# Moving the layer norm's factor from the output onto the queries, in a four-layer kernel on one core

## The chip, the core and the metric

The kernel runs on one core of a Trainium2 chip. The core has five engines with queues of their own: TensorE (PE in the profile, with its weight loads as PEld), VectorE (DVE), ScalarE (ACT), GpSimd (POOL) and SyncE (SP), which here only issues DMAs. The metric is the time on the device in microseconds, as the median of several runs.

## The reference

The input is a batch of 16 images of 4096 tokens (64 x 64) with 256 channels. Four layers follow each other, each as `x = x + layer(group_norm(x))`: a search in a codebook of 1024 entries, an attention along image rows with a sigmoid, a gate from a softmax over all tokens of an image, and a linear attention with a layer norm. The change concerns the last one:

```python
qkv = einsum('bxyc,cf->bxyf', x, w_qkv); q, k, v = split(qkv, 3)      # 4 heads of 32
q = softmax(q, over the 32) * 32 ** -0.5
k = softmax(k, over the 4096 tokens)
context = einsum('bhdn,bhen->bhde', k, v)
out = einsum('bhde,bhdn->bhen', context, q)
out = einsum('bxyh,hc->bxyc', out, w_out) + b_out
mu, var = mean and variance of out over the 256 channels
out = (out - mu) * rsqrt(var + 1e-3) * gamma + beta
```

The layer's result is added to its input, and the sum is the kernel's output.

## The kernel before

All work is cut into chunks of 512 tokens (`NCHUNK` = 8 chunks per image, `CH` = 4 tiles of 128 tokens per chunk). Each image goes through generators: `stats0` and `stage1` (the search), `layer1`, `rows2`, `stage2` and `gate2` (the gate), and `stage3` (the last layer). The generators of up to five images run interleaved. At the end of `tile_net_kernel` a heap of tasks decides the interleaving (L890 to L920): a task has a start, a length and a total, and each `yield n` of its generator moves it on by `length * n / total`. So an image's `stage3` is issued in pieces between the pieces of other stages of later images. Each engine works through its own queue in order, and one engine's wait holds all that is queued behind it, of whatever stage. SP issues most of the loads and stores, and its queue is in order too.

`stage3` has two loops over the chunks. The first (L740 to L801) makes the softmax of the keys, the context, and the queries. `queries` (L722) transposes the normalized queries of a chunk to 128 rows (4 heads x 32) by 512 tokens and stores them to DRAM. Between the loops (L803 to L827) the context is folded with `w_out` into one matrix of 128 x 256, `wctx`, whose second half carries gamma. Since `w_out` and the bias are centred over the channels in advance, the mean of the layer norm is zero. The variance of a token is then a quadratic form in its query, with the matrix `gram`.

The second loop (L854 to L882) is the output loop. Its parts are:

- `form(ch)` (L832) loads the transposed queries of a chunk again (L834, SP), multiplies them with `gram` (L836, PE) and multiplies the result by the queries (L838, DVE).
- `variance(ch)` (L840) sums over the 128 rows with four one-column matmuls (L844, PE), adds the epsilon (L846, ACT) and raises to the power -0.5 on POOL (L847). This gives the layer norm's factor, one number for each token, in `rss[ch]`, with the tokens along the partitions.
- For each pair of token tiles (`pr`), two products of queries and `wctx` go into one PSUM bank, `po` (L864). Each of the two is copied to the output tile `y` by ACT, which multiplies by the factor as a scale for each partition (L867).
- The residual input, stored with channels along the partitions, is transposed by PE into a second bank, `px` (L869), and a matmul of one row (L873) adds beta and what the group norm takes off.
- One pair later, DVE adds `px` to `y` (L875; the last one in L883), and SP stores a finished `y` (L878, L884).

Within the output loop a pair's step also carries the `form` (first pair) or the `variance` (second pair) of the next chunk.

PSUM is allocated from two pools: `ps_m` with four buffers of one bank each, which nearly all of the above draws from in turn (`bank`), and `ps_w` with two buffers of two banks. The queries' tile `qo` has three buffers, and `y` (tag `u4`) two.

Of the kernel before, what the change touches and what calls it, by code (L numbers as in the profile page):

```python
# [12 lines left out]
AF = mybir.ActivationFunctionType  # L13
ALU = mybir.AluOpType
AX = mybir.AxisListType

P = 128
C = 256
# [3 lines left out]
CH = 4  # L22
NCHUNK = NT // CH
# [18 lines left out]
def kernel(  # L42
# [7 lines left out]
    nc = tc.nc  # L50
# [17 lines left out]
    def bank(name):  # L68
        return ps_m.tile([P, 512], F32, tag="pm", name=name)
# [5 lines left out]
    ident = const.tile([P, P], F32, name="ident")  # L75
# [64 lines left out]
    def twice(row):  # L140
        return row.unsqueeze(1).to_broadcast([P, 2, C])
# [45 lines left out]
    for hf in range(2):  # L187
        pe = bank(f"pe_{hf}")
        for k in range(NK):
            nc.tensor.matmul(  # L190
                pe, lhsT=neg_mat, rhs=e_sq[:, k, hf * 512 : (hf + 1) * 512],
                start=(k == 0), stop=(k == NK - 1),
# [54 lines left out]
    for n in range(4):  # L247
        t = const.tile([P, 8], F32, name=f"m8_{n}")
# [450 lines left out]
    def stage3(b):  # L699
        tag = f"s3_{b}"  # L700
        dst = out[b].rearrange("(t p) c -> p t c", p=P)
        x3 = x3_d.pop(b)
        scale, nmean, xm_ = norm3.pop(b)
# [36 lines left out]
        for ch in range(NCHUNK):  # L740
# [23 lines left out]
            for pr in range(CH // 2):  # L764
                pqv = bank(f"pqv_{tag}_{ch}_{pr}").rearrange("p (j n) -> p j n", j=2)
                for j in range(2):
                    t = 2 * pr + j
                    for k in range(NK):
                        nc.tensor.matmul(  # L769
                            pqv[:, j, :], lhsT=xt[:, k, t * P : (t + 1) * P], rhs=wqv_n[:, k, :],  # L770
                            start=(j == 0 and k == 0), stop=False, skip_group_check=True,
# [33 lines left out]
        with tc.high_priority(offset=URGENT):  # L805
# [8 lines left out]
            wctx = wts.tile([P, 2, C], F32, tag="wctx", name=f"wctx_{tag}")  # L814
# [14 lines left out]
        queries(NCHUNK - 1)  # L829
        qs, prods, rss = {}, {}, {}  # L830

        def form(ch):  # L832
            qs[ch] = s3p.tile([P, CW], F32, tag="qo", name=f"qo_{tag}_{ch}", bufs=3)
            nc.sync.dma_start(out=qs[ch], in_=qTs[ch])  # L834
            pz = bank(f"pz_{tag}_{ch}")
            nc.tensor.matmul(pz, lhsT=gram, rhs=qs[ch], start=True, stop=True)  # L836
            prods[ch] = s3p.tile([P, CW], F32, tag="v2", name=f"qz_{tag}_{ch}", bufs=4)
            nc.vector.tensor_tensor(prods[ch], pz, qs[ch], ALU.mult)  # L838

        def variance(ch):  # L840
            prod = prods.pop(ch)
            pv = bank(f"pvr_{tag}_{ch}")
            for t in range(CH):
                nc.tensor.matmul(pv[:, t : t + 1], lhsT=prod[:, t * P : (t + 1) * P], rhs=one, start=True, stop=True)  # L844
            rss[ch] = small.tile([P, CH], F32, tag="ln_rs", name=f"lrs_{tag}_{ch}")
            nc.scalar.activation(rss[ch], pv[:, 0:CH], AF.Identity, bias=eps3)  # L846
            nc.gpsimd.tensor_tensor(rss[ch], rss[ch], mhalf, ALU.pow)  # L847

        form(0)
        yield 3  # L850
        variance(0)
        yield 3
        before = late = None
        for ch in range(NCHUNK):  # L854
            xt = xb.tile([P, NK, CW], F32, tag="xb", name=f"xo_{tag}_{ch}")
            nc.sync.dma_start(out=xt, in_=x3[ch])
            qT, rs = qs.pop(ch), rss.pop(ch)
            y = s3p.tile([P, CH, C], F32, tag="u4", name=f"y_{tag}_{ch}")
            for pr in range(2):
                po = bank(f"po_{tag}_{ch}_{pr}").rearrange("p (j c) -> p j c", c=C)  # L860
                px = bank(f"pxo_{tag}_{ch}_{pr}").rearrange("p (j c) -> p j c", c=C)
                for j in range(2):
                    t = 2 * pr + j
                    nc.tensor.matmul(  # L864
                        po[:, j, :], lhsT=qT[:, t * P : (t + 1) * P], rhs=wctx[:, 1, :], start=True, stop=True
                    )
                    nc.scalar.activation(y[:, t, :], po[:, j, :], AF.Copy, scale=rs[:, t : t + 1])  # L867
                    for k in range(NK):
                        nc.tensor.matmul(  # L869
                            px[:, j, k * P : (k + 1) * P], lhsT=xt[:, k, t * P : (t + 1) * P], rhs=ident,  # L870
                            is_transpose=True, start=(j == 0 and k == 0), stop=False, skip_group_check=True,
                        )
                nc.tensor.matmul(px, lhsT=ones3, rhs=twice(x_row), start=False, stop=True, skip_group_check=True)  # L873
                if late is not None:
                    nc.vector.tensor_tensor(late[1], late[0], late[1], ALU.add)  # L875
                late = px, y[:, 2 * pr : 2 * pr + 2, :]
                if pr == 1 and before is not None:
                    nc.sync.dma_start(out=dst[:, (ch - 1) * CH : ch * CH, :], in_=before)  # L878
                if ch + 1 < NCHUNK:
                    (form, variance)[pr](ch + 1)  # L880
                yield 3
            before = y  # L882
        nc.vector.tensor_tensor(late[1], late[0], late[1], ALU.add)  # L883
        nc.sync.dma_start(out=dst[:, TOK // P - CH :, :], in_=before)  # L884


# [28 lines left out]
    while queue:  # L915
        now, n = heapq.heappop(queue)
        _, length, gen, total = tasks[n]
# [39 lines left out]
```

## Time and profile before

| | |
|---|---|
| median of 3 runs | 5826.19 us (5826.03 to 5828.86) |
| profiled execution, its own time | 5832.41 us |
| span of the profiled execution | 5830.7 us |
| mean granted TensorE clock | 0.951 |
| DMA moved | 1059.49 MB, 182 GB/s over the span |
| `stage3` of the first image: first and last output addition | 1015.9 and 1114.0 us |
| output loop of the last image | 5784.3 us to the end |

The profiled execution is one run under the hardware profiler, and the times of single instructions come from it. A line of the groups reads: line of the kernel, engine, operation, output tile and input tiles, their shapes, how often; then busy us and mean ns of one; then the idle time of the engine just before these instructions, with what ended most of it. A line of the chain of work names the engine and the work that the end of the kernel was waiting for at that time. A line of the timeline has start, duration, engine, line, operation and tiles. A line of the waits names who waited for what: us in total, times, longest.

### The profile page before, as it was taken

The numbers are of one execution on the slowest core, as the hardware profiler recorded it, in microseconds if no ns is written. First come the engines' busy times: TensorE is split into PE (matmuls) and PEld (weight loads), VectorE is DVE, ScalarE is ACT, GpSimd is POOL, SyncE is SP. The second block draws the span as 40 slices with busy tenths as digits, with TensorE's granted clock in tenths as the row PEclk, the third lists the DMA queues.
The fourth block names the chain that finished last, engine by engine and source line by source line (L and its number), as shares of the span: only waits on it lengthen the run. The fifth ranks groups of instructions, "written<-read, shape, count | busy, mean of one in ns | idle before, by whom it ended". The sixth has DMA issues, their size and how long they took to land.

```text
span 5830.7 us, 79945 instructions
## 1 busy us (share of the span) xinstructions
PE 5289.1 (91%) x28463; PEld 3208.3 (55%) x28463; DVE 5145.4 (88%) x7282; ACT 4565.2 (78%) x6754; POOL 1956.8 (34%) x1314
## 2 busy tenths in 40 slices
PE   8978899889999999999999999999999999987778
PEld 3534455545656556565655656565565655564555
DVE  6489798899999999999999989999998999998883
ACT  4477597878878787887878788787888878888873
POOL 3123234223343333433333343332424334331332
PEclk9988999989999999999999999999999999998889
DMA  6443746555665656566565656657565664644543
GB/s 186 140 150 107 254 112 192 188 166 173 199 195 179 224 155 210 180 199 202 175 221 166 205 188 199 204 161 231 160 206 178 197 215 137 217 163 173 189 145 127
DMA packets 521381, 1059.49 MB, mean 182 GB/s; under 512 B 52504, under 2 KB 266392, under 8 KB 512792
## 3 DMA queue, kind: packets, MB, share of 16 engines
q1 hardware_dynamic: 406288, 885.11, 44.8%
q0 software_dynamic: 73728, 67.14, 8.0%
q10 hardware_dynamic: 40968, 102.13, 4.7%
q8 instruction: 226, 3.70, 0.3%
q14 instruction: 171, 1.40, 0.1%
HBM read 751.18 MB, written 303.04 MB: 181 GB/s over the span
## 4 chain that ended last, share of the span: by engine, by line
PE 36%; DVE 18%; ACT 12%; issue 5%; DMA 4%; POOL 3%; ACTq 0%; SPq 0%; POOLq 0%; DVEq 0%
PE pd_s L387 11%; DVE ex_s L630 8%; ACT ex_s L627 5%; PE po_s L864 3%; PE ph_l L477 3%; PE po_l L515 2%; PE pqv_s L769 2%; PE pk_s L747 2%; DVE i_s L398 2%; POOL qv_s L789 2%; PE pz_s L836 2%; PE pvr_s L844 1%; DVE nn_s L393 1%; PE pxo_s L869 1%; ACT nn_s L382 1%
## 5 line engine op out<-in xcount | busy, mean ns | idle before, releaser
L630 DVE CUSTOM_DVE_ANT_0 ex_s<-ex_s,x2b 128x2048 f32<-128x2048 f32 x1024 | 2392.9, 2343 | 73.4 <-ACT ex_s L627 72.8
L627 ACT ACTIVATE ex_s<-x0b,nmax_s,x_r 128x2048 f32<-128x2048 f32 x1024 | 2138.4, 2089 | 49.1 <-DVE num_s L630 40.0
L387 PE MATMUL pd_s<-e,xn_s 128*128 128x512 f32 x4096 | 2007.4, 622 | 64.5 <-DVE m L393 53.2
L399 POOL DMA_INDIRECT xc_s<-in_emb_rows,i_s x512 | 1121.4, 2190 | 1785.4 <-DVE i_s L398 1188.4
L387 PEld LDWEIGHTS pd_s<-e,xn_s 128*128 128x128 f32 x4096 | 760.2, 198 | 822.3 <-issue 681.3
L393 DVE CUSTOM_DVE_ANT_0 nn_s<-pd_s,nn_s 128x1024 f32<-128x1024 f32 x512 | 619.9, 1212 | 190.2 <-PE pd_s L387 91.7
L398 DVE FIND_INDEX8 i_s<-m,nn_s 128x8 uint32<-128x1024 f32 x512 | 623.0, 1217 | 0.1
L382 ACT ACTIVATE nn_s<-ne,nx_s 128x1024 f32<-128x1024 f32 x512 | 581.8, 1143 | 43.6 <-DVE nx_s L353 20.6
L477 PE MATMUL ph_l<-wh_l,xt_l 128*128 128x256 f32 x2048 | 533.4, 395 | 17.9 <-DVE m L393 12.5
L769 PE MATMUL pqv_s<-wqv_s,xk_s 128*128 128x256 f32 x2048 | 490.2, 381 | 0.0
L477 PEld LDWEIGHTS ph_l<-wh_l,xt_l 128*128 128x128 f32 x2048 | 382.0, 194 | 137.8 <-issue 64.4
L769 PEld LDWEIGHTS pqv_s<-wqv_s,xk_s 128*128 128x128 f32 x2048 | 389.3, 191 | 120.1 <-issue 58.0
L847 POOL TENSOR_TENSOR lrs_s<-lrs_s,mhalf 128x4 f32<-128x4 f32 x128 | 165.5, 1293 | 746.2 <-ACT lrs_s L846 720.1
L867 ACT ACTIVATE y_s<-po_s,lrs_s 128x256 f32<-128x256 f32 x512 | 239.1, 472 | 186.7 <-PE po_s L864 128.2
L864 PE MATMUL po_s<-wctx_s,qo_s 128*128 128x256 f32 x1024 | 335.1, 417 | 32.0 <-ACT y_s L867 30.5
L789 POOL TENSOR_TENSOR qv_s<-qv_s,qm_s 128x512 f32<-128x512 f32 x128 | 202.4, 1581 | 353.7 <-DVE qm_s L788 185.0
L515 PE MATMUL po_l<-at_l,h_l 64*128 64x64 f32 x4096 | 308.8, 286 | 7.5 <-DVE m L393 4.9
L515 PEld LDWEIGHTS po_l<-at_l,h_l 64*128 64x128 f32 x4096 | 272.1, 194 | 75.4 <-issue 37.1
L738 POOL TENSOR_TENSOR qv_s<-qv_s,qd_s 128x512 f32<-128x512 f32 x128 | 210.6, 1645 | 281.8 <-DVE qd_s L737 151.5
L864 PEld LDWEIGHTS po_s<-wctx_s,qo_s 128*128 128x128 f32 x1024 | 177.0, 198 | 175.6 <-ACT y_s L867 85.4
L332 ACT ACTIVATE xn_s<-xt_s,nb_n,s_n 128x512 f32<-128x512 f32 x256 | 200.7, 808 | 73.5 <-PE pd_s L387 48.5
L747 PE MATMUL pk_s<-xk_s,wk_s 128*128 128x512 f32 x512 | 253.3, 618 | 1.5 <-DMA xk_s<-x_g 1.2
(200 smaller groups left out, 7451.9 us busy)
## 6 DMA issues: line engine op xcount, KB each, us to landing
xs_s<-in_xT SPq DMA_DIRECT2D x128, 512.0 KB
xt_s<-in_xT SPq DMA_DIRECT2D x128, 512.0 KB
xc_s<-in_x SPq DMA_DIRECT2D x128, 512.0 KB
x_s<-xt_s ACTq DMA_DIRECT2D x128, 512.0 KB
xt_l<-x_s SPq DMA_DIRECT2D x128, 512.0 KB
x_l<-xt_l SPq DMA_DIRECT2D x128, 512.0 KB
xr_r<-x_l SPq DMA_DIRECT2D x128, 512.0 KB
xg_g<-x_l SPq DMA_DIRECT2D x128, 512.0 KB
```

The source lines that it names most:

```text
L382: nc.scalar.activation(nn, ne2, AF.Identity, bias=nx2[ch][:, t : t + 1])
L387: nc.tensor.matmul(pd[:, cols], lhsT=xn[ch][:, k, t * P : (t + 1) * P], rhs=e2[:, k, cols], start=(k == 0), stop=(k == NK - 1),)
L393: nc.vector.tensor_tensor_reduce(out=nn, in0=pd, in1=nn, scale=1.0, scalar=-3.0e38, op0=ALU.add, op1=ALU.max, accum_out=m8[:, 0:1],)
L398: nc.vector.max_index(i8, m8, nn)
L399: nc.gpsimd.indirect_dma_start(out=xc[ch][:, t, :], out_offset=None, in_=emb_rows, in_offset=bass.IndirectOffsetOnAxis(ap=i8[:, 0:1], axis=0),
L477: nc.tensor.matmul(ph[:, t, :], lhsT=X[:, k, t * P : (t + 1) * P], rhs=wh_n[:, k, :], start=(t % 2 == 0 and k == 0), stop=False, skip_grou ...
L515: nc.tensor.matmul(po[:, r, k * CH + t, :], lhsT=h[rows, t, k * P : (k + 1) * P], rhs=at[rows, t, :], start=True, stop=True,)
L627: nc.scalar.activation(ex, x0b, AF.Exp, bias=nmax[:, T : T + 1], scale=x01[:, T, 1:2], accum_out=den[:, h, T : T + 1])
L630: nc.vector.tensor_tensor_reduce(out=ex, in0=ex, in1=x2b, scale=1.0, scalar=0.0, op0=ALU.mult, op1=ALU.add, accum_out=num[:, h, T : T + 1],)
L747: nc.tensor.matmul(pk, lhsT=wk_n[:, k, :], rhs=xt[:, k, :], start=(k == 0), stop=(k == NK - 1))
L769: nc.tensor.matmul(pqv[:, j, :], lhsT=xt[:, k, t * P : (t + 1) * P], rhs=wqv_n[:, k, :], start=(j == 0 and k == 0), stop=False, skip_group ...
L864: nc.tensor.matmul(po[:, j, :], lhsT=qT[:, t * P : (t + 1) * P], rhs=wctx[:, 1, :], start=True, stop=True)
```

## The change

The factor is no longer a scale in the eviction of the products. A new function, `deviate`, spreads it: four PE transposes of a column broadcast over 128 columns give a bank in which each token's factor stands in all 128 rows, and DVE multiplies the queries by that bank. The products, the transposes of the residual and the row then go into one bank, as one accumulation, and ACT copies it to `y` in one instruction per pair. The additions on DVE are gone.

The loading of the queries becomes a function of its own, `fetch`, which runs three chunks ahead of the outputs; `form` and `variance` run two chunks ahead, and `deviate` one. Ahead of the loop stand three loads, two forms, two variances and one `deviate`, with steps between them. `qs` keeps its three buffers.

```diff
-        def form(ch):
+        def fetch(ch):
             qs[ch] = s3p.tile([P, CW], F32, tag="qo", name=f"qo_{tag}_{ch}", bufs=3)
             nc.sync.dma_start(out=qs[ch], in_=qTs[ch])
+
+        def form(ch):
             pz = bank(f"pz_{tag}_{ch}")
...
+        def deviate(ch):
+
+            rs = rss.pop(ch)
+            pd = bank(f"pdv_{tag}_{ch}")
+            for t in range(CH):
+                nc.tensor.transpose(pd[:, t * P : (t + 1) * P], rs[:, t : t + 1].to_broadcast([P, P]), ident)
+            nc.vector.tensor_tensor(qs[ch], pd, qs[ch], ALU.mult)
+
+        fetch(0)
+        fetch(1)
         form(0)
         yield 3
         variance(0)
-        yield 3
-        before = late = None
+        fetch(2)
+        yield 2
+        form(1)
+        yield 2
+        deviate(0)
+        variance(1)
+        yield 2
+        before = None
         for ch in range(NCHUNK):
             xt = xb.tile([P, NK, CW], F32, tag="xb", name=f"xo_{tag}_{ch}")
             nc.sync.dma_start(out=xt, in_=x3[ch])
-            qT, rs = qs.pop(ch), rss.pop(ch)
+            qT = qs[ch]
             y = s3p.tile([P, CH, C], F32, tag="u4", name=f"y_{tag}_{ch}")
             for pr in range(2):
-                po = bank(f"po_{tag}_{ch}_{pr}").rearrange("p (j c) -> p j c", c=C)
+                if pr == 1 and ch + 1 < NCHUNK:
+                    deviate(ch + 1)
                 px = bank(f"pxo_{tag}_{ch}_{pr}").rearrange("p (j c) -> p j c", c=C)
                 for j in range(2):
                     t = 2 * pr + j
-                    nc.tensor.matmul(
-                        po[:, j, :], lhsT=qT[:, t * P : (t + 1) * P], rhs=wctx[:, 1, :], start=True, stop=True
-                    )
-                    nc.scalar.activation(y[:, t, :], po[:, j, :], AF.Copy, scale=rs[:, t : t + 1])
                     for k in range(NK):
                         nc.tensor.matmul(
                             px[:, j, k * P : (k + 1) * P], lhsT=xt[:, k, t * P : (t + 1) * P], rhs=ident,
                             is_transpose=True, start=(j == 0 and k == 0), stop=False, skip_group_check=True,
                         )
+                for j in range(2):
+                    t = 2 * pr + j
+                    nc.tensor.matmul(
+                        px[:, j, :], lhsT=qT[:, t * P : (t + 1) * P], rhs=wctx[:, 1, :], start=False, stop=False,
+                        skip_group_check=True,
+                    )
                 nc.tensor.matmul(px, lhsT=ones3, rhs=twice(x_row), start=False, stop=True, skip_group_check=True)
-                if late is not None:
-                    nc.vector.tensor_tensor(late[1], late[0], late[1], ALU.add)
-                late = px, y[:, 2 * pr : 2 * pr + 2, :]
-                if pr == 1 and before is not None:
-                    nc.sync.dma_start(out=dst[:, (ch - 1) * CH : ch * CH, :], in_=before)
-                if ch + 1 < NCHUNK:
-                    (form, variance)[pr](ch + 1)
+                nc.scalar.copy(y[:, 2 * pr : 2 * pr + 2, :], px)
+                if pr == 0:
+                    if ch + 2 < NCHUNK:
+                        form(ch + 2)
+                else:
+                    if ch + 2 < NCHUNK:
+                        variance(ch + 2)
+                    if ch + 3 < NCHUNK:
+                        fetch(ch + 3)
+                    if before is not None:
+                        nc.sync.dma_start(out=dst[:, (ch - 1) * CH : ch * CH, :], in_=before)
                 yield 3
             before = y
-        nc.vector.tensor_tensor(late[1], late[0], late[1], ALU.add)
         nc.sync.dma_start(out=dst[:, TOK // P - CH :, :], in_=before)
```

## The prediction

> **What bounds the kernel now.** I read the busy shares first, then one stretch in the middle, then the chain of work that ended last, then the groups of the output loop, then that loop instruction by instruction.
>
> ```profile
> PE 5289.1 (91%) x28463; PEld 3208.3 (55%) x28463; DVE 5145.4 (88%) x7282; ACT 4565.2 (78%) x6754; POOL 1956.8 (34%) x1314
> ...
> 2700.00:3000.00 300.00, 283.48 (x1622) 178.36 (x1621) 280.83 (x401) 251.40 (x377) 109.46 (x72) 0.98 0.60 187
> ```
>
> The second line is one 300 us stretch: busy us of PE, weight loads, DVE, ACT, POOL, then granted clock, DMA share, GB/s. PE and DVE both look 94% busy, ACT 84%. For PE that overstates the load. The Trainium skill ("Perfetto Trace Analysis", section Identifying the Most-Contended Engine) says that matmul busy time is a poor measure because matmuls overlap in the pipeline, and that the occupancy of VectorE is a fair one. The trace agrees: a 512-column fp32 pass of L387 is listed with 622 ns, but eight in a row take 3.43 us in the chain, 0.43 us each. At such paces PE's work is 4864 passes of 512 columns x 0.43 = 2092 us, 5120 of 256 columns x 0.216 (eight of L477 in 1.73 us) = 1106 us, and about 1300 us of small ones (5376 of up to 128 columns at 0.11 = 590, the rest the narrow products of attention and the rows): 4500 us, 77% of the span. By the busy row PE binds and every added matmul lengthens the kernel; by the pace DVE is the fullest queue, and PE has room that is lost in waits. I take the pace.
>
> ```profile
> PE 36%; DVE 18%; ACT 12%; issue 5%; DMA 4%; POOL 3%; ACTq 0%; SPq 0%; POOLq 0%; DVEq 0%
> ```
>
> The chain changes engines all the time; no engine alone sets the end. These shares name 78% of the span, so I weigh time saved on PE by 36/78 = 0.46, on DVE by 0.23, on ACT by 0.15. That is my choice of a rule for a kernel of coupled queues.
>
> ```profile
> L864 PE MATMUL po_s<-wctx_s,qo_s 128*128 128x256 f32 x1024 | 335.1, 417 | 32.0 <-ACT y_s L867 30.5
> L867 ACT ACTIVATE y_s<-po_s,lrs_s 128x256 f32<-128x256 f32 x512 | 239.1, 472 | 186.7 <-PE po_s L864 128.2
> L875 DVE TENSOR_TENSOR y_s<-pxo_s,y_s 128x512 f32<-128x512 f32 x240 | 163.0, 680 | 34.1 <-ACT y_s L867 33.6 <-PE pxo_s L873 0.3
> L838 DVE TENSOR_TENSOR qz_s<-pz_s,qo_s 128x512 f32<-128x512 f32 x128 | 87.6, 685 | 75.0 <-PE pz_s L836 73.2 <-DMA qo_s<-qd_s 1.6
> L774 ACT COPY qv_s<-pqv_s 128x512 f32<-128x512 f32 x256 | 142.9, 576 | 39.5 <-PE pqv_s L773 39.3
> ```
>
> The last two figures of a line are the idle time before the group and its main cause. The output loop is a ping-pong: product (PE), scaled eviction (ACT), the next product into the other half of the same bank, eviction again. Both sides wait for each other. In the chain it looks like this:
>
> ```profile
> 2584.84 0.45 PE po_s L864 x2
> 2585.29 0.02 issue
> 2585.31 0.48 ACT y_s L867
> 2585.80 0.04 issue
> 2585.84 0.71 PE po_s L864 x2
> ```
>
> Two passes of a product at full pace take 0.43 us; after such a wait they take 0.6 to 0.7.
>
> **The change part by part.** There are 16 batches x 8 chunks = 128 chunks.
>
> *DVE.* The 256 residual additions go (L875 163.0 + L883 10.8 = 173.8 us). In come 128 products of spread factor and queries, 512 columns with one operand in PSUM, which is L838's shape: 128 x 685 ns = 87.7 us. Work: -86 us. The wait of 33.6 us for ACT goes. The new product waits for its transposes: nothing at best, 75 us at worst (L838's own wait on PE). The transposes stand well before their use, so I take the middle, 37. DVE: -86 - 34 + 37 = -83 us.
>
> *ACT.* The 512 scaled evictions go (239.1 us work, 186.7 us idle before them). In come 256 plain copies of 512 columns out of PSUM, L774's shape: 256 x 576 ns = 147.5 us, with L774's wait of 39.5. ACT: -92 work, -147 waiting, -239 us. Its wait for the POOL power (32.5 us in 25 cases) goes to PE.
>
> *PE.* The products, residual transposes and row are the same instructions, into one bank. Added are four transposes a chunk, 512 in all. The residual transposes give the pace:
>
> ```profile
> 5641.46 0.60 PE L869 MATMUL pxo_s<-ident,xo_s 128*128 128x128 f32 x4
> 5641.90 0.38 PE L873 MATMUL pxo_s<-x_row,ones 128*128 128x512 bf16 x1
> ```
>
> Four start 0.44 us before the next instruction, so 0.11 us each and 512 x 0.11 = +56 us. A broadcast column as weights is not in the trace; if nothing overlapped it would be 512 x 0.288 (mean of the transposes L362) = 147 us. I take 56, the same instruction but for the operand's step. Removed are PE's waits for the evictions: 30.5 on L864, 8.5 on L869, 5.7 on L836, 2.9 on L844 = 48 us, and the restart of the pipeline behind them: in the output phase from 2540 to 2660 us ten products take 0.6 to 0.7 instead of 0.43, about 2.1 us a batch, 34 us in all. New are two waits. The factor's transposes wait for POOL's power, which stands in its queue behind gathers that wait for DVE's indices; behind the transposes every PE instruction of all stages is held. ACT lost 32.5 us to this, with one step less of lead. And each chunk's first product waits for DVE's multiplication; PE lost 5.6 us to the like from L838. Ends 6 and 38; I take 25, nearer to what was seen since DVE's queue is full. PE: +56 - 48 - 34 + 25 = -1 us.
>
> *One bank.* The skill ("Perfetto Trace Analysis", section Matmuls) wants independent matmul groups to rotate through different banks, so that eviction overlaps the next group. That speaks against putting product and residual together: nothing of the bank can be read before its last pass. By the rule I would add a wait for each pair, at L774's 39.5/256 = 0.15 us, 39 us on ACT, already counted above; by the trace, the separate bank was no help, since PE waited 48 us on it. The changed loop takes five banks a chunk from the four-bank pool (2 outputs, form, variance, spread) where it took six, and an output bank is freed by its copy instead of by an addition a step later. I count no gain for it.
>
> *Queries and SP's queue.* The same 128 loads of 256 KB are issued, no more. But the buffer has three tiles, and a chunk's tile is now needed a step earlier: load c+3 waits until PE has finished with chunk c, and its form follows one step later, not three. SP is in order; behind the load stand the output store and other stages' loads. SP waits there already:
>
> ```profile
> SPq L834 <- PE po_s L864: 147.8, 52, 9.9
> ```
>
> In the changed program's order the PE work between the last product of chunk c and the form of c+3, at the paces above, has a median of 5.1 us and is under 4 us in 21 of 80 cases (never under 2.5). In the last batch before, a load issued at 5805.31 had landed when its form ran at 5807.10, so 1.8 us does when the DMA is free. I cost it at nothing; what hides it is that PE work, and rival 2 is what it costs if a load takes longer.
>
> *The ends.* In the last batch nothing else runs. A chunk takes 5.25 us (output stores at 5801.30, 5806.55). After: 8 transposes 0.87, 4 products 1.72, 2 rows 0.43, form 0.86, variance 0.80, spread 0.44 = 5.12 us plus restarts, no gain. The extra link ahead of the first chunk (transposes 0.44, product 0.69, handovers) costs 1.5 to 2 us, and the last DVE addition of 0.68 goes. I put +1.
>
> *Sum.* PE -1 x 0.46 = 0; DVE -83 x 0.23 = -19; ACT -239 x 0.15 = -36; ends +1: -54 us. The profiled execution took 5832.4 us (span 5830.7 and 1.7 around it), so its counterpart is about 5778; against the median, 5826.2 - 54 = 5772. I say 5775.
>
> **The rivals.**
>
> 1. *DVE alone binds.* In its favour: 94% real occupancy in the stretch above. Then its -86 of work and -34 of wait count fully: 5826 - 120 = 5706, or 5743 with the new wait of 37. Against it: only 18% of the chain.
>
> 2. *The query load becomes the wait (slower).* If loads land later than the 5.1 us of work that covers them, PE stops at the form, and with it the searches and attention queued behind. 5 forms a batch are exposed, 80 in all. A lateness of s us costs 80 x s x 0.46; the gain of 54 is gone at s = 1.5 us, and at s = 2.5 (a load of 7.6 us in a loaded queue) it gives 5772 + 92 = 5864. For it: SP's waits of up to 9.9 us on L834 and a DMA share of 0.6. Against it: DVE waited for this load once, 1.6 us.
>
> 3. *The room isn't used.* PE holds the pace of the output phase, where the chain is PE nearly throughout, and PE gains nothing (-1 by my sum): DVE and ACT just idle longer, 5826. Were the new PE waits 38 and not 25, PE would be at +12 and the time 5832.
>
> That the change does nothing at all is excluded: instructions of three engines differ.
>
> **How the numbers follow.** Forecast 0.53 (5745 to 5800), rival 1 0.13 (5700 to 5745), rival 3 0.14 (5810 to 5838), rival 2 0.20 (5835 to 5890). Less than 0.2%, 12 us, is no difference that a measurement of this kernel can tell. Faster: 0.53 + 0.13 and a little of rival 3, 0.67; same 0.12; slower 0.21. The range for 8 in 10 goes from 5710, inside rival 1, to 5850, inside rival 2; the forecast's own is 5745 to 5800.
>
> **What would show it.** The group of copies that replaces L867 with about 148 us busy and under 60 idle; the additions gone, and 128 multiplications near 685 ns; transposes of the factor at 0.11 us; PE's waits on y gone, and on the power or the multiplication under 40 us together; DVE's busy time near 5060, ACT's near 4475. I am wrong if PE waits at the form for the queries' DMA, if the transposes take 0.28 us, or if DVE's and ACT's busy time falls as worked out and the span doesn't.

## The result and the profile after

| | before | after |
|---|---|---|
| median of 4 runs | 5827.52 us (5826.03 to 5838.07) | 5757.54 us (5753.26 to 5760.43) |
| ratio of the times, 95% interval | | 0.9878 (0.9865 to 0.9892) |
| span of the profiled execution | 5830.7 us | 5758.7 us |
| busy: PE, DVE, ACT | 5289.1, 5145.4, 4565.2 us | 5245.1, 5067.1, 4496.9 us |

The kernel became 1.2% faster, about 71 us. The forecast was 5775, a gain of some 54 us. Size and sign were right, but the sum behind them was not: the experiments show that several of its terms had the wrong size, and that they offset each other.

These are the busy shares of the changed kernel and the shares of its chain of work, both from its page.

```profile
PE 5245.1 (91%) x28975; PEld 3212.6 (56%) x28975; DVE 5067.1 (88%) x7154; ACT 4496.9 (78%) x6498; POOL 1930.8 (34%) x1314
...
PE 40%; DVE 16%; ACT 9%; DMA 5%; issue 5%; POOL 3%; ACTq 0%; DVEq 0%; SPq 0%; POOLq 0%
```

And this is the middle stretch, 2700 to 3000 us, in the changed kernel.

```profile
2700.00:3000.00 300.00, 282.56 (x1655) 174.82 (x1654) 280.47 (x390) 248.16 (x361) 103.96 (x69) 0.98 0.62 196
```

DVE's busy time is down by 78.3 us, where 86 of work were forecast, and ACT's by 68.3, where 92 were (90.0 in the sums of the groups, whose instructions overlap in part). The kernel is still one of coupled queues, with PE at 94% and DVE at 93% of the stretch. DMA's share of the chain has gone from 4% to 5%, and the chain's list by line names one load for 3% of the span: that of the queries. The groups of the output loop say where; the first line is the form of the kernel before, the others are of the changed kernel:

```profile
L836 PE MATMUL pz_s<-qo_s,gram_s 128*128 128x512 f32 x256 | 143.7, 645 | 6.1 <-ACT y_s L867 5.7 <-ACT gram_s L827 0.2 <-DVE y_s L875 0.2
...
L895 ACT COPY y_s<-pxo_s 128x512 f32<-128x512 f32 x256 | 149.1, 583 | 164.8 <-PE pxo_s L894 146.2 <-issue 10.3 <-ACT ex_s L627 3.5
L890 PE MATMUL pxo_s<-wctx_s,qo_s 128*128 128x256 f32 x1024 | 268.5, 385 | 0.0
L857 DVE TENSOR_TENSOR qo_s<-pdv_s,qo_s 128x512 f32<-128x512 f32 x128 | 87.5, 684 | 24.7 <-PE pdv_s L856 24.7
L856 PE MATMUL pdv_s<-ident,lrs_s 128*128 128x128 f32 x512 | 82.0, 284 | 5.9 <-POOL lrs_s L849 5.9
L838 PE MATMUL pz_s<-qo_s,gram_s 128*128 128x512 f32 x256 | 147.8, 661 | 40.8 <-DMA qo_s<-qd_s 39.7 <-ACT y_s L895 0.7 <-ACT gram_s L827 0.2
L840 DVE TENSOR_TENSOR qz_s<-pz_s,qo_s 128x512 f32<-128x512 f32 x128 | 87.7, 685 | 112.3 <-PE pz_s L838 112.3
```

Read against the lines of before (those of the prediction, and L836): the products (L890, before L864) no longer wait at all, and one pass lasts 385 ns where it lasted 417. The copies (L895) have the work that was expected, but still wait 164.8 us, against 186.7 for the evictions before; under 60 was forecast. The form (L838, before L836) now waits 39.7 us for the load of its queries, where it waited 6.1 us in all and never for that load. And DVE's multiplication behind the form (L840, before L838) waits 37 us longer.

The last image shows the new wait on its own. This is the chain of work there:

```profile
5719.05 4.34 DMA qo_s<-qd_s
5723.40 0.14 issue
5723.53 1.10 PE pz_s L838 x2
5724.63 0.44 PE pdv_s L856 x4
5725.07 0.44 PE pxo_s L884 x4
5725.50 0.86 PE pxo_s L890 x4
5726.37 0.03 PE pxo_s L894
5726.40 4.14 DMA qo_s<-qd_s
```

It is a closed ring: the last products of a chunk free a query tile, the load into it takes its time, the form waits for the load, and behind the form on PE stand the next products, which free the next tile. The chain runs through five such loads in this image, of 4.05, 4.34, 4.14, 3.63 and 2.67 us. From one of them to the next a chunk takes 6.63 to 7.35 us (7.35 from 5719.05 to 5726.40), against 5.25 before.

Where the 72 us between the two profiled executions lie can be read from the one DVE instruction an image that masks the folded context (L809). From the 2nd to the 12th image its period is 343.96 us before and 338.56 after, 5.4 us less for each image. From the 12th to the 16th, where no new images start, before takes 851.4 us and after 839.6; from there to the end it is 54.0 before and 60.4 after. So the part from the 2nd to the 12th image, the steady part from here on, gained 54 of the 72 us, what lies ahead of it 12.6, the last images 11.8, and the very end lost 6.4.

### The profile page after: what moved, and what is told of

It is laid out like the page before. It is cut to its first block, busy times and chain, and to the rows that moved or that the text cites. A ratio compares the mean times of both kernels' runs of the same rounds, so it can differ in the third digit from the quotient of the medians.

```text
span 5758.7 us, 80501 instructions
## 1 busy us (share of the span) xinstructions
PE 5245.1 (91%) x28975; PEld 3212.6 (56%) x28975; DVE 5067.1 (88%) x7154; ACT 4496.9 (78%) x6498; POOL 1930.8 (34%) x1314
## 4 chain that ended last, share of the span: by engine, by line
PE 40%; DVE 16%; ACT 9%; DMA 5%; issue 5%; POOL 3%; ACTq 0%; DVEq 0%; SPq 0%; POOLq 0%
PE pd_s L387 12%; DVE ex_s L630 7%; ACT ex_s L627 4%; PE ph_l L477 3%; PE pxo_s L890 3%; DMA qo_s<-qd_s 3%; PE po_l L515 2%; PE pqv_s L769 2%; PE pk_s L747 2%; PE pz_s L838 2%; POOL qv_s L789 2%; PE pxo_s L884 2%; DVE i_s L398 2%; DVE nn_s L393 1%; PE pvr_s L846 1%
## 5 line engine op out<-in xcount | busy, mean ns | idle before, releaser
L399 POOL DMA_INDIRECT xc_s<-in_emb_rows,i_s x512 | 1097.6, 2144 | 1846.2 <-DVE i_s L398 1361.2
L387 PEld LDWEIGHTS pd_s<-e,xn_s 128*128 128x128 f32 x4096 | 747.2, 196 | 816.6 <-issue 680.7
L477 PE MATMUL ph_l<-wh_l,xt_l 128*128 128x256 f32 x2048 | 520.6, 392 | 15.1 <-DVE m L393 10.0
L515 PEld LDWEIGHTS po_l<-at_l,h_l 64*128 64x128 f32 x4096 | 258.8, 192 | 59.4 <-issue 28.1
L515 PE MATMUL po_l<-at_l,h_l 64*128 64x64 f32 x4096 | 286.8, 281 | 5.4 <-DVE m L393 2.8
L895 ACT COPY y_s<-pxo_s 128x512 f32<-128x512 f32 x256 | 149.1, 583 | 164.8 <-PE pxo_s L894 146.2
L890 PE MATMUL pxo_s<-wctx_s,qo_s 128*128 128x256 f32 x1024 | 268.5, 385 | 0.0
L362 PE MATMUL pt_s<-ident,xc_s 128*128 128x128 f32 x1024 | 159.5, 287 | 99.2 <-DMA xc_s<-in_emb_rows,i_s 66.6
```

Source lines behind the costliest of these rows:

```text
L387: nc.tensor.matmul(pd[:, cols], lhsT=xn[ch][:, k, t * P : (t + 1) * P], rhs=e2[:, k, cols], start=(k == 0), stop=(k == NK - 1),)
L399: nc.gpsimd.indirect_dma_start(out=xc[ch][:, t, :], out_offset=None, in_=emb_rows, in_offset=bass.IndirectOffsetOnAxis(ap=i8[:, 0:1], axis=0),
L477: nc.tensor.matmul(ph[:, t, :], lhsT=X[:, k, t * P : (t + 1) * P], rhs=wh_n[:, k, :], start=(t % 2 == 0 and k == 0), stop=False, skip_grou ...
L515: nc.tensor.matmul(po[:, r, k * CH + t, :], lhsT=h[rows, t, k * P : (k + 1) * P], rhs=at[rows, t, :], start=True, stop=True,)
L890: nc.tensor.matmul(px[:, j, :], lhsT=qT[:, t * P : (t + 1) * P], rhs=wctx[:, 1, :], start=False, stop=False, skip_group_check=True,)
```

## The experiments

Every kernel was timed against the kernel before on the same chip. For comparison the ratios are turned into microseconds of a kernel of 5828 us:

| kernel | ratio, 95% interval | us against before |
|---|---|---|
| after | 0.9878 (0.9865 to 0.9892) | -71 |
| after, multiplied queries in a tile of their own | 0.9824 (0.9808 to 0.984) | -103 |
| after, second multiplication | 1.0175 (1.0153 to 1.0197) | +102 |
| after, one copy of a chunk twice | 0.9893 (0.9866 to 0.9919) | -62 |
| after, copies one pair later | 0.9905 (0.9885 to 0.9925) | -55 |
| after, form and variance half a chunk later | 0.9945 (0.9928 to 0.9961) | -32 |
| after, without the spread | 0.9843 (0.9823 to 0.9863) | -92 |
| before, products ahead of evictions | 1.0015 (1.0004 to 1.0025) | +9 |
| before, 112 of 256 additions left out | 0.9957 (0.994 to 0.9973) | -25 |
| before, one plain eviction a pair | 1.0024 (1.0014 to 1.0035) | +14 |
| before, the longer lead alone | 1.0068 (1.0044 to 1.0093) | +40 |
| before, one bank, no factor | 0.9699 (0.9678 to 0.972) | -175 |
| before, additions turned into ACT copies | 0.9831 (0.981 to 0.9852) | -98 |

The intervals are 6 to 15 us wide to either side, so that a difference of two lines is known to some 10 to 20 us. The mean granted clock also differs between the lines, and the last section says what that leaves open for the small differences.

**Is it the query tile?** The multiplied queries go into a tile of their own; all else stays.

```diff
-            nc.vector.tensor_tensor(qs[ch], pd, qs[ch], ALU.mult)
+            qT = s3p.tile([P, CW], F32, tag="v2", name=f"qd_{tag}_{ch}", bufs=4)
+            nc.vector.tensor_tensor(qT, pd, qs[ch], ALU.mult)
+            qs[ch] = qT
```

> The changed kernel with one edit: the multiplied queries go into a tile of their own, so a query buffer is free for the next load as soon as DVE has multiplied, a chunk earlier than when PE has used it. Nothing else differs. Both theories expect PE's waits at the form for the queries' DMA (39.7 us in 36 waits) to go, and the last image's chunks to fall from 7.3 us to about 5.4, which alone is 14 us. Theory A (coupled queues, each engine's time counts by its share of the chain, PE 0.46): 14 + 0.46 x 25 further us, so about 5732. Theory B (DVE alone binds wherever images overlap): only the 14 us of the last image, about 5743.

Measured: 5724.93 us (5722.15 to 5737.31). The form and the copies of this kernel:

```profile
L838 PE MATMUL pz_s<-qo_s,gram_s 128*128 128x512 f32 x256 | 144.3, 647 | 1.1 <-ACT y_s L897 0.6 <-ACT gram_s L827 0.4
L897 ACT COPY y_s<-pxo_s 128x512 f32<-128x512 f32 x256 | 148.8, 582 | 142.0 <-PE pxo_s L896 120.9 <-issue 11.9 <-ACT ex_s L627 3.5
L840 DVE TENSOR_TENSOR qz_s<-pz_s,qo_s 128x512 f32<-128x512 f32 x128 | 87.5, 684 | 64.4 <-PE pz_s L838 62.7 <-PE pxo_s L896 1.6
```

A load's buffer is now freed by DVE's multiplication and no longer by the products a chunk later. The wait of 39.7 us is gone, DVE's wait behind the form is 64.4 instead of 112.3 us, and the kernel is some 31 us (give or take 12) faster than the changed one. In the last image a chunk takes 5.18 us (forms at 5699.55, 5704.72, 5709.90). So the query load did cost time, about 31 us, and this version is the fastest of those that leave nothing out. It is still 73 us behind the kernel below that has one bank, the old lead and no spread.

**Is it the ping-pong between product and eviction?** In the kernel before, both products of a pair are issued ahead of both scaled evictions; the work is the same.

```diff
+                for j in range(2):
+                    t = 2 * pr + j
                     nc.scalar.activation(y[:, t, :], po[:, j, :], AF.Copy, scale=rs[:, t : t + 1])
+                for j in range(2):
+                    t = 2 * pr + j
```

> The kernel before with one edit: both products of a pair are issued ahead of the two scaled evictions, so PE no longer waits for ACT between them. Work on every engine is unchanged. Theory A: PE loses 82 us of waits and restarts (x 0.46 = 38), ACT 88 of its 128 us of waiting (x 0.15 = 13), DVE some 20 of its 34 (x 0.23 = 5): about 5771. Theory B (DVE's time alone counts): only DVE's 20 to 34 us of waiting, 5793 to 5807. If the ping-pong cost nothing because PE had the room: 5827.

Measured: 5837.28 us, 0.15% slower. The waits inside the pair have gone and come back elsewhere:

```profile
L864 PE MATMUL po_s<-wctx_s,qo_s 128*128 128x256 f32 x1024 | 296.5, 409 | 11.8 <-ACT fg_l L473 7.5 <-ACT y_s L869 3.5 <-ACT s_n L277 0.4
L836 PE MATMUL pz_s<-qo_s,gram_s 128*128 128x512 f32 x256 | 139.2, 627 | 15.3 <-ACT y_s L869 13.9 <-ACT at_l L502 0.6 <-ACT lrs_s L846 0.4
L844 PE MATMUL pvr_s<-one,qz_s 128*128 128x1 f32 x1024 | 128.1, 246 | 16.8 <-ACT y_s L869 13.2 <-DVE qz_s L838 3.6
```

The products wait 3.5 us for the evictions (30.5 before), but form and variance wait 13.9 and 13.2 us for them, where it was 5.7 and 2.9. Taking the ping-pong apart brought no gain by itself.

**Does DVE alone set the pace?** In the kernel before, the additions at the first pair of each chunk are left out (112 of 256), so nearly half of the residual is missing.

```diff
-                if late is not None:
+                if late is not None and pr == 1:
```

> The kernel before, leaving out half of its residual additions (those of the second pair of each chunk but the last), 120 x 0.68 = 82 us of DVE work, as much as the change takes off DVE. The output lacks the residual there. The ping-pong stays. Theory A: (82 + about 16 of waiting) x 0.23 = 23, about 5804. Theory B (DVE alone binds): the full 82 to 98, 5729 to 5745.

Measured: 5804.6 us, -25. The edit takes out 112 additions and not the 120 of the expectation, 76 us of DVE work (112 x 680 ns). The gain is near what DVE's weight of the forecast gives, and far from a kernel that DVE alone binds. The steady period was 345.4 us, no shorter than the 344.0 of before: the gain came outside the steady part.

**Twice the new work on DVE.** The changed kernel gets a second multiplication for each chunk.

```diff
+            waste = s3p.tile([P, CW], F32, tag="v2", name=f"waste_{tag}_{ch}", bufs=4)
+            nc.vector.tensor_tensor(waste, pd, qs[ch], ALU.mult)
             nc.vector.tensor_tensor(qs[ch], pd, qs[ch], ALU.mult)
```

> The changed kernel with a second multiplication of the spread factor and the queries into a tile that nobody reads: 128 more DVE instructions of 684 ns, +87.5 us of DVE work, nothing else. Weighted sum (DVE at its share of the chain, 0.23): 5757 + 20 = 5777. If DVE binds alone: 5757 + 87 = 5844. If DVE's work is free, because PE and ACT set the pace of the steady stretch, as leaving out half of the additions of the kernel before suggested: under 5765.

Measured: 5933.65 us. None of the three was right: 87.5 us of work cost some 173 (give or take 15) against the changed kernel.

```profile
L838 PE MATMUL pz_s<-qo_s,gram_s 128*128 128x512 f32 x256 | 154.0, 686 | 92.7 <-DMA qo_s<-qd_s 90.0 <-ACT sq_s L335 2.1 <-ACT gram_s L827 0.3
L897 ACT COPY y_s<-pxo_s 128x512 f32<-128x512 f32 x256 | 148.2, 579 | 308.9 <-PE pxo_s L896 251.5 <-issue 54.5 <-ACT lrs_s L848 1.2
```

The form's wait for the queries rose from 39.7 to 90.0 us and the products waited 19.9 us for the multiplication. The extra instruction stands ahead of the products that free the query tile, so it lengthens the ring. These two waits are some 70 of the 173 us; what the rest is, was not separated, and the granted clock of 1500 to 4800 us was 0.96 where the changed kernel had 0.98. Half of the additions moved the time by 0.3 of their work, this instruction by twice its work: one weight for DVE does not fit both.

**Twice a copy on ACT.** The first pair's copy is done twice.

```diff
+                if pr == 0:
+                    nc.scalar.copy(y[:, 2 * pr : 2 * pr + 2, :], px)
                 nc.scalar.copy(y[:, 2 * pr : 2 * pr + 2, :], px)
```

> The changed kernel with the first pair's copy of each chunk done twice: 128 more ACT copies of 583 ns, +75 us of ACT work, and the bank of that pair is held 0.6 us longer. Theory A (the weighted sum, ACT at its chain share of 0.15): 5757 + 11 = 5768. Theory B (ACT's 92 us of work are what gave the 48 us that DVE's work doesn't explain, a weight of about 0.5): 5757 + 39 = 5796 or more. Theory C (what counts is how long the output banks are held): the hold of one bank in five grows by 0.6 us, a small part of the step by which the late addition held it before: under 5770.

Measured: 5765.4 us, some 9 us (give or take 17) for 75 us of ACT work, at the clock of the changed kernel (0.958 in the mean of the runs of either). A weight of 0.5 is out.

**Less work on ACT alone.** In the kernel before, one plain copy takes both products of a pair.

```diff
-                    nc.scalar.activation(y[:, t, :], po[:, j, :], AF.Copy, scale=rs[:, t : t + 1])
+                nc.scalar.copy(y[:, 2 * pr : 2 * pr + 2, :], po)
+                for j in range(2):
+                    t = 2 * pr + j
```

> The kernel before with both products of a pair evicted by one plain ACT copy of 512 columns in place of two scaled ones of 256; it leaves out the layer norm's factor. ACT's work falls by 92 us as in the change, the additions on DVE and the two output banks stay as they were. Theory A (ACT's work at 0.15; the waits were shown to be worth nothing): 5828 - 14 = 5814. Theory B (ACT's work at about 0.5): 5828 - 48 = 5780. Theory C (the banks): no gain from ACT's work, 5820 to 5830.

Measured: 5841.8 us, 0.24% slower, though ACT's busy time fell from 4565.2 to 4500.7 us and this edit takes the ping-pong out as well. No theory had that. Less work on ACT alone brought no gain. But this kernel ran at a mean granted clock of 0.944, the one before on the same chip at 0.951, so it is not shown that ACT's work would be worth nothing at an equal clock (see the last section).

**A bank held longer.** In the changed kernel each copy is issued one pair later, as the addition was.

```diff
...
-                nc.scalar.copy(y[:, 2 * pr : 2 * pr + 2, :], px)
+                if late is not None:
+                    nc.scalar.copy(late[0], late[1])
+                late = y[:, 2 * pr : 2 * pr + 2, :], px
...
+        nc.scalar.copy(late[0], late[1])
```

> The changed kernel with each copy of a finished output bank issued one pair later, as the residual addition stood one pair later in the kernel before. Every engine does the same work; an output bank, one of the four of its pool, is held a step longer. Theory C (the shorter hold of banks is what gave the 48 us): 5757 + 30 to 50 = 5787 to 5807. Theories A and B (only work counts): 5752 to 5765; ACT waits less for its bank.

Measured: 5769.7 us, some 16 us (give or take 14) slower than the changed kernel. If holding a bank for a step more has a price, it is below the 30 to 50 us of that theory.

**The lead alone.** The kernel before with the change's order of loads, forms and variances. The lines left out split `fetch` from `form` and set the order ahead of the loop, as in the change.

```diff
...
-                if ch + 1 < NCHUNK:
-                    (form, variance)[pr](ch + 1)
+                if ch + 2 < NCHUNK:
+                    (form, variance)[pr](ch + 2)
+                if pr == 1 and ch + 3 < NCHUNK:
+                    fetch(ch + 3)
```

> The kernel before with the change's order of loads, forms and variances alone (loads three chunks ahead, form and variance two), while the scaled evictions, the two banks and the additions stay. No engine's work changes. Theory L (the earlier form and variance are what gave the 48 us that DVE's work doesn't explain): 5828 - 48 = 5780. Theory S (the lead only serves the spread; what counts is that evictions and additions go): 5828, or up to 5850 where the query load now waits for its buffer, as it does in the changed kernel.

Measured: 5872.68 us, 40 us slower, with the new wait in the form:

```profile
L838 PE MATMUL pz_s<-qo_s,gram_s 128*128 128x512 f32 x256 | 155.7, 693 | 45.6 <-DMA qo_s<-qd_s 38.3 <-ACT y_s L876 5.9 <-ACT ex_s L627 1.3
```

By itself the lead is a cost and not a gain.

**The change without its spread.** `deviate` and its calls are left out.

```diff
-        def deviate(ch):
...
-        deviate(0)
...
-                if pr == 1 and ch + 1 < NCHUNK:
-                    deviate(ch + 1)
```

> The changed kernel without the spread: no transposes of the factor, no multiplication of the queries. It leaves out the layer norm's factor. PE -56 us, DVE -87.5 us, one bank a chunk fewer. By the weights of the prediction: 5757 - 56 x 0.46 - 88 x 0.23 = 5711. If the spread stands on the path that frees the query tiles, as the doubled multiplication suggested (it cost 176 us): 5757 - 88 - 30 (the query wait) = 5640 or less.

Measured: 5740.65 us, only some 20 us (give or take 14) less than the changed kernel, where 46 and more were expected.

```profile
L838 PE MATMUL pz_s<-qo_s,gram_s 128*128 128x512 f32 x256 | 147.0, 658 | 34.8 <-DMA qo_s<-qd_s 34.3
L884 ACT COPY y_s<-pxo_s 128x512 f32<-128x512 f32 x256 | 148.4, 580 | 157.7 <-PE pxo_s L883 144.2 <-DMA xo_s<-x_g 6.5 <-ACT lrs_s L848 4.7
```

The wait for the queries is still 34.3 us without the spread, so the spread isn't its main cause. This kernel too ran at a lower clock than the one it is compared with, 0.951 against 0.958, so the 20 us are no price of the spread at an equal clock.

**One bank with the old lead.** The kernel before, with product, residual and row in one bank and one copy.

```diff
-                po = bank(f"po_{tag}_{ch}_{pr}").rearrange("p (j c) -> p j c", c=C)
...
-                    nc.scalar.activation(y[:, t, :], po[:, j, :], AF.Copy, scale=rs[:, t : t + 1])
...
+                    nc.tensor.matmul(
+                        px[:, j, :], lhsT=qT[:, t * P : (t + 1) * P], rhs=wctx[:, 1, :], start=False, stop=False,
+                        skip_group_check=True,
+                    )
...
-                if late is not None:
-                    nc.vector.tensor_tensor(late[1], late[0], late[1], ALU.add)
-                late = px, y[:, 2 * pr : 2 * pr + 2, :]
+                nc.scalar.copy(y[:, 2 * pr : 2 * pr + 2, :], px)
```

> The kernel before, its forms and variances one chunk ahead as there, with product, residual and row in one bank, one plain copy a pair and no additions. It leaves out the layer norm's factor. DVE -174 us, ACT -92 us, four banks a chunk where there were six. Theory S (the evictions and additions are the gain; DVE at 0.27 as half of the additions showed, ACT at 0.1): 5828 - 47 - 9 = 5772; if DVE's and ACT's relief only work together: under 5740. Theory L (the gain is the lead's): 5772 or above.

Measured: 5665.12 us, -175. Tried alone, half of the additions had given -25, the plain eviction +14 and the products ahead of the evictions +9: together the parts give much more.

```profile
L875 ACT COPY y_s<-pxo_s 128x512 f32<-128x512 f32 x256 | 147.6, 580 | 88.6 <-PE pxo_s L874 86.9 <-DMA out<-y_s 0.6 <-ACT u_g L684 0.5
L836 PE MATMUL pz_s<-qo_s,gram_s 128*128 128x512 f32 x256 | 136.1, 614 | 0.1
L870 PE MATMUL pxo_s<-wctx_s,qo_s 128*128 128x256 f32 x1024 | 270.9, 388 | 0.0
```

With the old lead the form waits for nothing, and the copies 88.6 us instead of 164.8 (157.7 with the longer lead and no spread). A chunk of the last image takes 4.74 us (forms at 5644.12, 5648.86).

**A lead half a chunk shorter.** In the changed kernel the form of chunk c+2 comes after the second pair of chunk c and no longer after the first, its variance after the first pair of c+1, and the load of its queries at the start of c, a step earlier against its form.

```diff
-        fetch(2)
...
-        variance(1)
...
+            if ch + 2 < NCHUNK:
+                fetch(ch + 2)
...
                 if pr == 0:
-                    if ch + 2 < NCHUNK:
-                        form(ch + 2)
+                    if ch + 1 < NCHUNK:
+                        variance(ch + 1)
                 else:
                     if ch + 2 < NCHUNK:
-                        variance(ch + 2)
-                    if ch + 3 < NCHUNK:
-                        fetch(ch + 3)
+                        form(ch + 2)
```

> The changed kernel with the form and the variance half a chunk later (the form of chunk c+2 after the second pair of c, its variance after the first pair of c+1, its spread as in the change) and the load of its queries half a chunk earlier against its form, so that it finds its buffer free. All work is that of the changed kernel; only the order of stage3's pieces differs. If the query load is all that the longer lead costs: 5757 - 30 = 5727, as with a tile of its own. If the longer lead costs the 80 us that stand between the two kernels without the factor: 5757 - 80 = 5677.

Measured: 5797.27 us, some 39 us slower than the changed kernel; both expectations failed.

```profile
L838 PE MATMUL pz_s<-qo_s,gram_s 128*128 128x512 f32 x256 | 143.0, 642 | 0.2 <-ACT gram_s L827 0.2
L856 PE MATMUL pdv_s<-ident,lrs_s 128*128 128x128 f32 x512 | 87.6, 297 | 70.3 <-POOL lrs_s L849 70.3
L857 DVE TENSOR_TENSOR qo_s<-pdv_s,qo_s 128x512 f32<-128x512 f32 x128 | 87.4, 683 | 94.9 <-PE pdv_s L856 94.9
```

The wait for the queries is gone (0.2), but the spread now stands one step behind its variance, not two, and PE waits 70.3 us for POOL's power (5.9 in the changed kernel). By the L809 of the two profiled executions the steady period is that of the changed kernel (338.3 us, 338.6 there); the loss lies behind it, in the last images (867.3 us from the 12th to the 16th, 839.6 there). So this shorter lead is no cheaper than the long one, and it trades one wait for another.

**The additions moved to ACT.** The kernel before with one plain copy of both products, and an ACT copy over `y` in the place of each addition. The six banks and their late release stay.

```diff
-                    nc.scalar.activation(y[:, t, :], po[:, j, :], AF.Copy, scale=rs[:, t : t + 1])
+                nc.scalar.copy(y[:, 2 * pr : 2 * pr + 2, :], po)
...
-                    nc.vector.tensor_tensor(late[1], late[0], late[1], ALU.add)
+                    nc.scalar.copy(late[1], late[0])
...
```

> The kernel before with one plain ACT copy for both products of a pair, and with the late addition on DVE replaced, at its place, by a late ACT copy of the residual bank over y. It leaves out the factor and the products' share of the sum. DVE -174 us, ACT +57 us, PE the same, six banks a chunk held as before. If DVE's relief as a whole is what gives the 175 us of the one-bank kernel: 5660 to 5690. If it is the banks (four a chunk, each free after its copy): 5780 to 5830. If the weights add up as half of the additions, the plain eviction and the doubled copy showed: 5828 - 48 + 14 + 6 = 5800.

Measured: 5723.55 us, -98, between all three.

```profile
L867 ACT COPY y_s<-po_s 128x512 f32<-128x512 f32 x256 | 149.4, 584 | 85.9 <-PE po_s L864 83.3 <-DMA out<-y_s 1.2 <-PE pxo_s L875 0.8
L877 ACT COPY y_s<-pxo_s 128x512 f32<-128x512 f32 x240 | 140.0, 586 | 3.4 <-PE pxo_s L875 0.7
```

Taking DVE's 174 us away helps by 98 even with 57 us more on ACT. Against the plain eviction, from which this kernel differs only in the additions, it is 112, with a mean clock of 0.952 for 0.944. The other 77 us (give or take 17) of the one-bank kernel come with 149 us less on ACT, two banks fewer a chunk and no late release. By the doubled copy (9 for 75) ACT's work would be some 18 of them, and by the late copy the hold some 16; what the rest is, was not separated.

**Where in the kernel the gains lie.** L809 shows it, in one profiled execution of each kernel. The steady period is 344.0 us before, 345.4 with half of the additions left out, 348.4 with the plain eviction, 338.6 in the changed kernel, 338.3 without the spread, 337.3 with the tile of its own, 336.2 with the additions on ACT and 336.1 with one bank. So the two kernels without additions on DVE and without the lead are alike in the steady part, whatever their banks and ACT's work. What parts these two profiled executions, 42.5 us, lies nearly all between the 12th and the 16th image (792.4 us with one bank, 831.4 with the additions on ACT).

## Why the forecast was right in size and wrong in its sum

The difference of 71 us is made up like this, from the table: one bank with one copy and no additions -175; the longer lead on top of it +84; the spread on top of that +20. These are differences of whole kernels, each with its own clock. The forecast was made of other pieces, and it had no term for the clock.

- **DVE, -83 x 0.23 = -19.** The work came as said (-78 by the busy row), the multiplication's own wait was 24.7 for 37, and 37 us were added to DVE's wait behind the form, which the sum lacked: DVE's idle time in all went from 685 to 692 us, so the -34 of removed waiting was given back. The weight is what failed. It nearly held for the 112 additions (-25 for 76, a weight of 0.33), but the whole of them, carried by ACT, gave 98 for 174, a weight of 0.56, or 0.65 with the 112 us against the plain eviction. A share of the chain was used as a constant, and it isn't one.
- **ACT, -239 x 0.15 = -36, two thirds of the forecast gain.** The step that failed is the -147 of waiting: the copies wait 164.8 us and not 39.5, so 22 us fell away instead of 147. L774's wait was the wrong row to borrow, and not for the length of its bank's group: its eight passes and row take 1.95 us in the chain (1.73 and 0.22), the output bank's four transposes, four passes of products and row 1.53 (0.44, 0.87 and 0.22). What the wait goes with is the lead: 88.6 us with the old one, 157.7 with the longer one and no spread, 142.0 where the form no longer waits for the queries. Why a copy waits longer under the longer lead was not found. There is also an error of kind: the idle time before a group was counted as time to be gained. In all ACT is idle for 1262 us after the change and was for 1265 before (span less busy time); what fell away at the copies came back elsewhere. The -92 of work is right (-90.0 by the groups), but no run shows a gain from it alone: +14 in the kernel before, at a lower clock, and 75 us added cost some 9.
- **PE, -1.** The products lost 98.6 us (66.6 of work by the profile's modelled ends and 32.0 idle), more than the 82 forecast for all waits and restarts. The transposes take 0.44 us for four in the chain, the 0.11 us each that was taken. The new waits for the power and the multiplication were 5.9 and 0.0 us, below the 25 and just below its lower end; the run with a shorter lead shows that the fear of POOL's power was sound, with 70.3. What the term lacks is the form's 39.7. That the removed waits were a gain at all is not borne out: with the products ahead of the evictions the kernel before was no faster.
- **One bank, no gain counted.** The rule of the Trainium skill ("Perfetto Trace Analysis", section Matmuls) that groups should rotate through banks, which spoke against this part, was not given a price, and no loss from breaking it showed: the kernel with one bank and half of the ACT copies was 77 us faster than the one with two banks held and the additions on ACT. So "no gain" may have been too little; how much of the 77 us is the banks' own remains open, and in the steady part of the two profiled executions there is nothing to share out.
- **Queries and SP's queue, costed at nothing.** This is the step that was plainly wrong. It rested on a load "issued at 5805.31" that "had landed when its form ran at 5807.10". The two don't belong together. In the last image of before, the last loads and forms are these:

```profile
5800.06 0.32 SPq L834 DMA_DIRECT2D qo_s<-qd_s  x1
5805.31 0.32 SPq L834 DMA_DIRECT2D qo_s<-qd_s  x1
5810.56 0.32 SPq L834 DMA_DIRECT2D qo_s<-qd_s  x1
...
5807.10 1.02 PE L836 MATMUL pz_s<-qo_s,gram_s 128*128 128x512 f32 x2
5812.35 1.02 PE L836 MATMUL pz_s<-qo_s,gram_s 128*128 128x512 f32 x2
5817.60 1.02 PE L836 MATMUL pz_s<-qo_s,gram_s 128*128 128x512 f32 x2
```

  Counted from the end, the load of 5805.31 is the last but one, and so is the form of 5812.35: 7.0 us lay between them, and nothing could be said about 1.8. In the last image of the changed kernel the load takes 2.67 to 4.34 us where it is waited for, against the forecast's cover of 5.1 in the median and under 4 in a quarter of the cases. Rival 2 thus described what happens, but not its amount: 39.7 us over 80 forms are 0.5 us each, and its own rule makes 18 us of that. Taking the wait away gained some 31. It does not make the longer lead free: the kernel with a tile of its own stays 73 us behind the one with the old lead and no spread, and the spread's 20 us are only part of that.
- **The ends, +1.** Behind the 16th L809 the end is 6.4 us later. The 5.12 us for a chunk was right for the work, as the 5.18 of the kernel with its own tile shows; the ring with the load makes it 6.6 to 7.35.

Rival 1 (DVE alone) fell with the half additions, rival 3 (the room isn't used) with the result. Too little for DVE's relief as a whole and perhaps for the banks, too much for ACT's waits, nothing for the query load and the rest of the lead's cost: the errors nearly cancelled. That the forecast's 5775 is 17 us from the measured time is luck in good part.

## What to carry to other kernels

When a step is moved ahead, follow each of its buffers to the instruction that frees it, and pair loads with their users by counting, not by nearness in time: here one more tile, taken from a pool that already existed, was worth another 31 us. In a kernel whose queues are all coupled, price an edit by undoing it together with its neighbours: half of an engine's relief gave 25 us, the whole 98, and the whole bundle 175, so a share of the chain of work is no price per microsecond. Nor is idle time before a group a gain in waiting: ACT's whole idle time stayed at 1265 and 1262 us. A lead buys one wait and may sell another: measure both (70.3 us for the power on one side, 39.7 us for the queries on the other).

## What was not expected of the hardware

A column of four-byte numbers broadcast over 128 columns costs as much as an ordinary operand of a transpose: L856 has a mean of 284 ns and a weight load of 142 ns, the residual's transposes L884 284 and 150 ns. Four of them take 0.44 us in the chain, as the residual's do. The forecast had kept 0.288 us each, with nothing overlapped, open as an upper end.

Between executions of one and the same kernel the time goes with the granted clock: the five runs of the kernel with its own tile took 5737.3, 5733.4, 5724.9, 5722.3 and 5722.2 us at 0.954, 0.956, 0.957, 0.958 and 0.959. In the 27 runs of the kernel before that stand beside the plain eviction, a fitted line gives 4.4 us less for each 0.001 more of clock, and in the other kernels with five runs and more 1.7 to 7.

Between kernels the mean clock differs too: 0.9509 before, 0.9583 after, 0.9444 with the plain eviction, 0.9490 with the products ahead, 0.9510 without the spread, 0.9568 with one bank. At 4 us for 0.001, an estimate from those lines, some 30 of the 71 us gained would go with the clock, as would some 26 us of loss in the plain eviction and some 29 without the spread: at an equal clock these two would be about 12 us faster than before and about 50 faster than the changed kernel. Whether the clock is a cause here, or follows from how PE's work and waits fall, no run shows. So +14, +9 and +20 are no prices of ACT's work, the ping-pong and the spread by themselves. The large differences stand: the clock would make some 25 of the 175 us of the one-bank kernel, and the kernel with its own tile is faster than the changed one at the same clocks of 0.957 to 0.959 (5722.2 to 5724.9 us against 5753.3 to 5760.4).
